# Gated cross-attention block: the turned query tile goes through memory instead of from SBUF to SBUF

## The chip, the cores and the metric

The kernel runs on one core of one Trainium2 chip. The metric is device time in microseconds (us) for one execution on that core. Three runs of the kernel before are given, and one further execution was taken by the hardware profiler. Engines are named as in the profile: PE (TensorE matmul), PEld (its weight loads), DVE (VectorE), ACT (ScalarE), POOL (GpSimd), SP (SyncE, which here only issues DMAs). All data is float32.

## The reference

There are 32 batches of 256 tokens with 256 features, and for each batch 77 context vectors. The first half of the block is a cross attention without softmax, with 8 heads of 128 features:

```python
f_q, f_k = proj(layernorm(x)), proj(ctx)           # heads x batch x tokens x 128; f_v is f_k
cosine   = f_q @ f_k.T / (|f_q| |f_k|)
variance = q_ratio * k_ratio                       # 2 min(var, 1) / (var + 1) of each feature vector
mixed    = cw * cosine + vw * cosine * decorr_scale + ww * variance
out      = (mixed @ f_v) @ w_out.T + b_out         # x += tanh(g_xattn) * out
```

The weights cw, vw, ww and decorr_scale are one number for each head, computed from all tokens. The second half is a self attention with 16 heads of 16 features, with the softmax over keys, two L2-normalised projections and a GELU, again gated and added to x.

To form f_q times f_k, PE needs both with the 128 features of a head on the partitions. Query features are made with tokens on the partitions, and so a tile of 128 tokens by 8 heads by 128 features has to be turned before it can be used.

## The kernel before

**Head.** The first part of the kernel (to about 170 us) reads all of x once for global statistics, prepares the weights and computes the first batches' features. Then comes a steady part, one cycle for each batch.

**Cycle.** A hand-written list names the stages of a cycle in their order; each entry says for which batch ahead of the current one a stage is run. The engines PE, ACT, DVE and POOL keep this order, since their instructions are recorded through a wrapper (line 30, which is why the profile puts nearly all work on L30). SP is not wrapped: a scheduler orders its DMAs by when their inputs are expected. The stages around the change, with n the cycle's batch:

```python
(2, turn_queries, 0),        # after mix_values(n, 1); then attend and ff_stats of n+1
(3, key_features),
(2, transpose_keys, 0),      # the reader of fv
(2, turn_queries, 1),        # near the end of the cycle
(3, measure_keys),
(3, align_keys),
(1, query_ratios),           # next cycle: n+2 is now n+1
(1, query_scores, 0),        # the reader of fqT: "mm<-fqT,fvT"
```

**Queries.** `query_features` makes fq, 128 tokens by 1024, for each of a batch's two token tiles (t = 0 and 1). `scale_queries` normalises it. `turn_queries` turns it into fqT, which has the 128 features of a head on the partitions. For the first two batches PE transposes; for the other 30, DVE transposes blocks of 32 by 32 into fb, and DMAs put the blocks in place: block row i of fb (partitions 32 i to 32 i + 31) and block column j go to partitions 32 j to 32 j + 31 of fqT. There is a single fqT buffer, and two buffers of fb. `query_scores` multiplies fqT by fvT; it needs both token tiles.

**Keys.** `key_features` computes key features in blocks of 128 context rows into one of four places of fvx, while a batch has 77 rows. So `align_keys` (lines 262 and 263) copies each batch's rows out of one or two blocks to partitions 0 to 76 of fv, by one DMA a piece, and their norms from nrx to nr:

```python
n = min(P - row, M - at)
nc.sync.dma_start(out=k["fv"][at : at + n], in_=fvx[i % 4][row : row + n])      # L262
nc.sync.dma_start(out=k["nr"][at : at + n], in_=nrx[row : row + n, i % 4, :])   # L263
```

The pieces have from 1 to 77 rows of 4 KB. There are two buffers of fv; a buffer's last reader is `transpose_keys` of the batch before the last ("mm<-dk,fv" in the trace).

**SP's queue.** All DMAs of the steady part are issued from SP, one after the other: the copies into fqT (L428), fv (L262), nr (L263), the output store of a batch (L626) and the load of x for a batch four ahead (L188). Eight semaphores are given out to the DMAs in turn, so SP issues a DMA only when the one eight places before it in that turn has landed.

Of the kernel before, what the change touches and what calls it, by code (L numbers as in the profile page):

```python
# [8 lines left out]
F32 = mybir.dt.float32  # L9
# [5 lines left out]
P = 128  # L15
H = 8
# [17 lines left out]
def gated_block_kernel(  # L34
# [24 lines left out]
    nc = tc.nc  # L59
# [8 lines left out]
    const = ctx.enter_context(tc.tile_pool(name="const", bufs=1))  # L68
    pa = ctx.enter_context(tc.tile_pool(name="pa", bufs=2))
    sw = ctx.enter_context(tc.tile_pool(name="sw", bufs=1))  # L70
    ps = ctx.enter_context(tc.tile_pool(name="ps", bufs=3, space=PSUM))
    ps_s = ctx.enter_context(tc.tile_pool(name="ps_s", bufs=2, space=PSUM))
    ps_z = ctx.enter_context(tc.tile_pool(name="ps_z", bufs=1, space=PSUM))
# [63 lines left out]
    def mm_tile():  # L137
        return ps.tile([P, 512], F32, tag="mm", name="mm")
# [263 lines left out]

    def turn_queries(b, t):

        k = kept[b]
        if t == 0:
            k["fqT"] = pa.tile([P, S // 32, H, 32], F32, tag="fqT", name="fqT", bufs=1)
        if b < 2:
            for hh in range(2):
                pt = mm_tile()  # L410
                for i in range(4):
                    h = hh * 4 + i
                    pe.transpose(
                        pt[:, i * P : (i + 1) * P], k["fq", t][:, h * P : (h + 1) * P], ident
                    )
                (act.copy if hh == 0 else dve.tensor_copy)(
                    k["fqT"][:, 4 * t : 4 * t + 4, hh * 4 : hh * 4 + 4, :],
                    pt.rearrange("p (h i a) -> p i h a", h=4, a=32),
                )
            return  # L420
        fb = pa.tile([P, 4, H, 32], F32, tag="fb", name="fb", bufs=2)
        dve.transpose(
            fb.rearrange("p j h a -> p h j a"),
            k["fq", t].rearrange("p (h j a) -> p h j a", j=4, a=32),
        )
        for i in range(4):
            for j in range(4):
                nc.sync.dma_start(  # L428
                    out=k["fqT"][32 * j : 32 * j + 32, 4 * t + i],
                    in_=fb[32 * i : 32 * i + 32, j],  # L430
                )

    def attend(b, t):

# [497 lines left out]
    for g in range(-2, NG):  # L932
# [9 lines left out]
        for i in range(4):  # L942
            k = 4 * g + i
# [179 lines left out]

    dve.tensor_scalar(dg[:, 1, :], ident[0:H, 0:H], lg[:, 2:3], 4.0, ALU.mult, ALU.mult)
    run(0, turn_queries, 0)
    pt = mm_tile()
    pe.matmul(
# [12 lines left out]
    for pair in (2, 0, 1):  # L1140
        run(0, key_outputs, pair)
    run(1, key_features)
    run(0, turn_queries, 1)
    run(0, query_ratios)
    for pair in range(3):
# [53 lines left out]
        (0, exponents, 2, 0),  # L1199
        (0, mix_values, 1),  # L1200
        (2, turn_queries, 0),
        (1, attend, 0),
        (1, ff_stats, 0),
# [69 lines left out]
```

## Time and profile before

| | |
|---|---|
| runs | 1469.19 us median of 3, from 1465.18 to 1469.28 |
| profiled execution | 1467.87 us, of which 1466.1 us is the span from first to last instruction |
| mean granted PE clock | 0.975 |
| issues of fqT<-fb on SP | 960 of 32 KB, median 589 ns on SP's queue |
| DVE transposes into fb | 60, median 1235 ns |
| matmuls on fqT or fvT (mm<-fqT,fvT) | 1024, median 379 ns |
| the SP queue's DMA share | 16.8% of 16 engines, 73.15 MB |

The page gives busy time by engine over the whole span, the chain of work that ended last, and the costliest groups of instructions. A busy share over the span is an average over the head and the steady part. More is told by windows that are cut at the same instruction of successive cycles, by the timelines of PE and SP in one such window, and by the list of who waited for whom. A wait for several semaphores is put down to the one that came last by the profile, so a DMA named there may stand for another DMA. The page prints no time to landing for these DMAs; where the text gives one, it is the last of the DMA's semaphore increments in the trace.

### The profile page before, as it was taken

To read this page: it belongs to the slowest core of one execution; us is meant where nothing else is said; L and a number is where in the kernel's file an instruction comes from. 1 tells how busy PE (TensorE), PEld (TensorE's weight loads), DVE (VectorE), ACT (ScalarE), POOL (GpSimd) and SP (SyncE) were. 2 spreads that over 40 slices of the span, in tenths; PEclk is the share of its full clock that TensorE was granted. 3 is DMA by queue.
4 is the path that set the end of the run, shared out by engine and by line. 5 is a ranking of instruction groups with operands and counts; after the bars stand their busy time and mean duration, and the time that the engine had idled before them with its cause. 6 is when DMAs were issued, how large, how long until landed. Compare 5 with 4: busy or idle time off the path is not lost.

```text
span 1466.1 us, 26809 instructions
## 1 busy us (share of the span) xinstructions
PE 1392.0 (95%) x8833; PEld 814.9 (56%) x8833; DVE 1057.0 (72%) x3053; ACT 905.5 (62%) x2978; POOL 533.4 (36%) x660
## 2 busy tenths in 40 slices
PE   6898899999999999999999899999999998999985
PEld 6764555555555555655555455555555554555541
DVE  5734678787777777777877686877878775878743
ACT  5712456667667666666666566766666664666675
POOL 5922333343333333343433233333433323333210
PEclk9989999999999999999999999999999998999996
DMA  8500011111111111111111111111111111111100
GB/s 267 176 15 27 3 45 46 42 51 43 49 47 49 46 54 47 59 49 40 51 43 45 42 49 49 56 46 51 45 44 49 47 41 40 47 42 35 32 19 15
DMA packets 72282, 74.87 MB, mean 51 GB/s; under 512 B 21370, under 2 KB 57135, under 8 KB 72142
## 3 DMA queue, kind: packets, MB, share of 16 engines
q1 hardware_dynamic: 71310, 73.15, 16.8%
q8 instruction: 70, 1.15, 0.3%
q14 instruction: 70, 0.57, 0.1%
q10 hardware_dynamic: 832, 0.00, 0.0%
HBM read 22.98 MB, written 8.39 MB: 21 GB/s over the span
## 4 chain that ended last, share of the span: by engine, by line
PE 69%; ACT 14%; DMA 4%; DVE 4%; issue 2%; SPq 1%; POOL 1%; ACTq 0%; POOLq 0%; DVEq 0%
PE mm L30 53%; PE sc L30 9%; ACT e L30 7%; PE zp L30 6%; ACT L30 4%; DMA fv<-fvx 4%; DVE nm L30 2%; SPq L428 1%; ACT u L30 1%; ACT fvx L30 1%; ACT dry L30 0%; ACT ge L30 0%; POOL rs L30 0%; DMA fqT<-fb 0%; DMA nr<-nrx 0%
## 5 line engine op out<-in xcount | busy, mean ns | idle before, releaser
L30 ACT ACTIVATE e<-sc,nm 128x256 f32<-128x256 f32 x1024 | 471.8, 484 | 200.5 <-DVE nm L30 200.4
L30 DVE TENSOR_REDUCE nm<-sc 128x4 f32<-128x1024 f32 x256 | 301.4, 1219 | 50.4 <-PE sc L30 50.4
L30 PE MATMUL mm<-winT,xTc 128*128 128x512 f32 x512 | 237.3, 605 | 2.6 <-DVE xTc L30 2.6
L30 ACT ACTIVATION_READ_ACCUMULATOR e<-sc,nm 128x1 f32 x1024 | 221.2, 216 | 0.0
L30 POOL TENSOR_TENSOR rq<-qt,nhalf 128x8 f32<-128x8 f32 x64 | 105.2, 1643 | 273.2 <-DVE qt L30 273.2
L30 PEld LDWEIGHTS mm<-winT,xTc 128*128 128x128 f32 x512 | 95.0, 191 | 120.7 <-issue 94.0
L30 PE MATMUL sc<-q,kTf 32*128 32x512 f32 x1024 | 153.9, 646 | 6.1 <-ACT e L30 6.1
L30 PE MATMUL mm<-vw,s 128*128 128x256 f32 x640 | 146.9, 384 | 0.0
L30 PE MATMUL zp<-e,vz 128*32 128x256 f32 x2048 | 140.0, 392 | 5.2 <-DVE vz L30 4.3
L30 POOL TENSOR_SCALAR i<-nn 128x2 f32<-128x2 f32 x64 | 14.0, 219 | 344.4 <-ACT ge L30 344.4
L30 PEld LDWEIGHTS mm<-vw,s 128*128 128x128 f32 x640 | 119.0, 190 | 28.5 <-issue 13.7
L30 POOL TENSOR_TENSOR fq<-fq,rq 128x1024 f32<-128x1024 f32 x64 | 121.3, 1896 | 5.0
L30 PE MATMUL mm<-w_of,zT 128*128 128x512 f32 x256 | 118.1, 605 | 0.8 <-DVE zT L30 0.8
L30 PEld LDWEIGHTS zp<-e,vz 128*32 128x32 f32 x2048 | 59.1, 111 | 95.7 <-issue 37.6
L30 PE MATMUL mm<-fqT,fvT 128*64 128x256 f32 (+2 forms) x1024 | 98.4, 396 | 13.2 <-DMA nr<-nrx 11.6
L30 DVE BATCH_NORM_STATS2 qst<-fq 128x6 f32<-128x128 f32 x512 | 104.7, 277 | 0.0
L30 PE MATMUL mm<-woutT,fvT 128*64 128x256 f32 (+2 forms) x1024 | 99.2, 384 | 0.6 <-DVE fvT L30 0.5
L30 POOL TENSOR_SCALAR rs<-mv 128x1 f32<-128x1 f32 x64 | 32.8, 512 | 169.5 <-DVE mv L30 135.4
L30 DVE RECIPROCAL sums<-sums 128x8 f32<-128x8 f32 x128 | 24.6, 192 | 92.6 <-ACT e L30 92.6
L30 ACT COPY vw<-mm 128x512 f32<-128x512 f32 x32 | 18.8, 586 | 115.6 <-PE mm L30 115.6
L30 PEld LDWEIGHTS mm<-fqT,fvT 128*64 128x64 f32 (+2 forms) x1024 | 48.7, 122 | 71.0 <-issue 51.9
L30 ACT ACT_TABLE_LOAD x64 | 82.1, 1283 | 7.4 <-DMA x<-in_x_dram 4.2
(204 smaller groups left out, 2316.8 us busy)
## 6 DMA issues: line engine op xcount, KB each, us to landing
fqT<-fb SPq DMA_DIRECT2D x960, 32.0 KB
x<-in_x_dram SPq DMA_DIRECT2D x64, 256.0 KB
out_dram<-x SPq DMA_DIRECT2D x32, 256.0 KB
fv<-fvx SPq DMA_DIRECT2D x13, 308.0 KB
ct<-in_ctx_dram SPq DMA_DIRECT2D x4, 512.0 KB
w_in_n<-in_L_xattn_w_in_dram SPq DMA_DIRECT2D x2, 512.0 KB
w_out_n<-in_L_xattn_w_out_dram SPq DMA_DIRECT2D x1, 1024.0 KB
ct<-in_ctx_dram SPq DMA_DIRECT2D x1, 384.0 KB
```

Of the source, the lines that this page charges most:

```text
L30: return lambda *args, **kw: self._tc.keep_in_program_order(method(*args, **kw))
L428: nc.sync.dma_start(out=k["fqT"][32 * j : 32 * j + 32, 4 * t + i], in_=fb[32 * i : 32 * i + 32, j],)
```

## The change

The blocks of fb no longer go straight to fqT. A pool of two buffers in memory (HBM) is added. Each tile is stored there in one DMA, fb with its 128 partitions by 4 KB as it lies, and is read back in four DMAs, one for each block column j: a read takes the 1 KB of column j of all 128 rows and lays row 32 i + p on partition p of the 32 partitions, at block i. The reads wait until the store has landed. The first two batches are as before. All else in the kernel's text is the same.

```diff
     sw = ctx.enter_context(tc.tile_pool(name="sw", bufs=1))
+    dram = ctx.enter_context(tc.tile_pool(name="dram", bufs=2, space=bass.MemoryType.DRAM))
...
             k["fq", t].rearrange("p (h j a) -> p h j a", j=4, a=32),
         )
-        for i in range(4):
-            for j in range(4):
-                nc.sync.dma_start(
-                    out=k["fqT"][32 * j : 32 * j + 32, 4 * t + i],
-                    in_=fb[32 * i : 32 * i + 32, j],
-                )
+        fd = dram.tile([P, 4, H * 32], F32, tag="fd", name="fd")
+        nc.sync.dma_start(out=fd, in_=fb.rearrange("p j h a -> p j (h a)"))
+        for j in range(4):
+            nc.sync.dma_start(
+                out=k["fqT"][32 * j : 32 * j + 32, 4 * t : 4 * t + 4].rearrange(
+                    "p i h a -> p i (h a)"
+                ),
+                in_=fd[:, j].rearrange("(i p) n -> p i n", p=32),
+            )
```

## The prediction

> **What bounds the kernel now.** I read the busy table first, then windows cut at the turns (from the end of one transpose into fb, t = 1, to the next), then the timelines of PE and SP where a cycle is long, and the chain there.
>
> ```profile
> PE 1392.0 (95%) x8833; PEld 814.9 (56%) x8833; DVE 1057.0 (72%) x3053; ACT 905.5 (62%) x2978; POOL 533.4 (36%) x660
> ```
>
> ```profile
> 724.33:764.29 39.96, 39.57 (x262) 22.91 (x261) 32.14 (x95) 26.46 (x89) 15.61 (x18) 1.00 0.17 50
> ...
> 805.10:851.64 46.54, 41.58 (x262) 23.78 (x261) 32.24 (x96) 26.57 (x89) 15.37 (x17) 0.93 0.15 45
> ...
> 1213.84:1263.72 49.88, 42.49 (x262) 24.12 (x261) 32.32 (x96) 26.57 (x89) 15.36 (x17) 0.90 0.12 37
> ```
>
> The columns are the window, its length, then busy time of PE, PEld, DVE, ACT and POOL, the granted clock, and DMA. An ordinary cycle is 39.96 us with PE busy 39.57 of it: nothing there can be won by a DMA. Two cycles of the same work take 46.54 and 49.88 us. In the longer one PE (first fence) stood idle 7.00 us before the first matmul on fqT, and SP (second) spent 20.01 us on the 16 copies of one tile, where 10 is usual:
>
> ```profile
> 1227.33 1.14 PE L30 MATMUL sc<-q,kTf 32*128 32x512 f32 x8
> 1235.47 5.52 PE L30 MATMUL mm<-fqT,fvT 128*64 128x256 f32 x32 [7.00 <-DMA nr<-nrx]
> ```
>
> ```profile
> 1199.60 11.22 SPq L428 DMA_DIRECT2D fqT<-fb  x16
> 1210.93 1.51 SPq L262 DMA_DIRECT2D fv<-fvx  x2
> 1213.87 20.01 SPq L428 DMA_DIRECT2D fqT<-fb  x16
> ```
>
> ```profile
> 1211.80 16.49 DMA fv<-fvx
> 1228.29 0.02 issue
> 1228.31 0.51 SPq L428
> ```
>
> The chain tells why: the second fv piece (71 rows) was 16.49 us under way, and the eighth copy went out only when it had landed at 1228.29. By the trace's semaphore increments the last copy landed at 1235.12, just ahead of PE's start, so PE waited for fqT; the nr that the row names landed after it (1235.85).
>
> The same two sources give every late turn (b of the queries that are turned):
>
> | b | slow fv piece, landed at | PE ready for fqT | PE waits | cycle longer by |
> |---|---|---|---|---|
> | 7 | 53 rows, 411.3 | 417.8 | 0.73 | 0.8 |
> | 12 | 74 rows | 619.1 | 0.04 | 0.1 |
> | 17 | 73 rows, 817.0 | 819.7 | 4.56 | 6.6 |
> | 19 | 47 rows, 899.1 | 906.1 | 0.88 | 0.9 |
> | 27 | 71 rows, 1228.3 | 1228.5 | 7.00 | 9.9 |
>
> Together 18.3 us. (Every fifth cycle, 40.81 us, has four matmuls more; that is work.) In the other turns the last copy lands 0.4 to 3.2 us before PE wants it.
>
> [...] 77 rows land in 3.4 us, 73 in 15.1, 47 in 10.7. [...] seven fqT copies issued behind the 71 rows, from 1213.87 on, land together between 1228.50 and 1229.60. [...] the granted clock is 0.93 and 0.90 in the two long cycles, and PE's busy time there is 2.0 and 2.9 us more for the same matmuls.
>
> **The change part by part.** The order of instructions on PE, ACT, DVE and POOL is the same in both programs; only SP's changes.
>
> *Removed:* 16 copies a tile, 60 tiles. Each holds SP 0.63 us (10.04 / 16), the last lands 1.84 us after its issue: 11.3 us from turn to landing, and SP is held for 10.
>
> *Added:* one store of 512 KB and four reads of 128 KB. Neither is in the trace; the nearest rows are an output store and the load that waits for it:
>
> ```profile
> 494.07 0.54 SPq L626 DMA_DIRECT2D out_dram<-x  x1
> 496.26 0.34 SPq L188 DMA_DIRECT2D x<-in_x_dram  x1
> ```
>
> The 256 KB store landed within 2.19 us. Loads of 256 KB in the head land 0.62 us apart, so twice the bytes make about 2.9 us (an estimate; bounds 2.2, and 6.5, which a 512 KB load of ct took in the crowded head). A 256 KB load alone lands 2.6 us after issue, a copy in 1.84, a load in the crowd in 3.5: I take 2.6 per read, bounds 1.8 and 3.5. Issues 0.6 us apart. Round trip: 2.9 + 0.1 + 3 x 0.6 + 2.6 = 7.4 us, with SP held for 5.4.
>
> *Moved, t = 0:* fqT of t = 0 has over 25 us of room, so its landing is worth nothing. But SP then goes on to fv, 4.6 us sooner, and now fv's own conditions decide. In the b = 27 cycle these are ACT's copies into fvx (start 1204.72, 1.03 long) for the first piece and PE's last reading of the old fv (1204.77, 1.92 long) for the second: 1206.7, where it was issued at 1211.80. Where there is one piece, only the second condition holds.
>
> *Moved, t = 1:* in cycles with two pieces the program puts both nr copies between store and reads. They wait for nrx, ready 4.2 us after the turn (POOL, 405.64 + 1.66 against 403.13), and take SP 1.6: reads begin at 5.9, land at 5.9 + 1.8 + 2.6 = 10.3. PE wants fqT about 14.5 us after the turn, so this is covered; were the cover gone, the cost would be the excess. The output store and x load behind it come no later than before (old release 10.1, new 8.3).
>
> *The late turns.* The store has 8 of its 128 rows on the engine that fv occupies[...]: 8/71 of 16.49 is 1.9 us, less the fixed part, 1.6. Then reads: 0.1 + 1.8 + 2.6 = 4.5. So fqT lands 6.1 us after fv, where the nine copies left took 6.8.
> - b = 27: fv lands 16.49 after 1206.7, 1223.2; fqT 1229.3; PE ready 1228.5: 0.8 us wait left, about 1.1 us with the slower clock.
> - b = 17: the same offset gives issue 797.9 instead of 801.94, fv 813.0, fqT 819.1 against 819.7: none.
> - b = 7: fv 407.5, fqT 413.6 against 417.8: none.
> - b = 19: one piece, issue about 883.9 instead of 888.45, fv 894.6, fqT 900.7 against 906.1: none.
> - b = 12: none.
>
> Gain 18.3 - 1.1 = 17.2 us. What is late next is PE itself. The DMA engines' load rises from 16.8% by 31 MB on 73: no bound. Against the profiled execution, 1467.87 us (span 1466.1 and 1.8 around it), this is 1450.7; the median shown, 1469.19, is 1.3 higher, so I predict 1451.
>
> **Rivals.**
> - *SP is not free sooner.* If store and reads of t = 0 hold SP for the old 10 us (store at its upper bound 6.5, and reads that issue slowly), fv stays where it was and only the tail shrinks from 6.8 to 6.1: b = 7, 12 and 19 are cured (1.8 us), b = 17 and 27 get 0.7 x 1.4 each: 3.8 us, 1464. For it: no such store is in the trace. Against: the 2.19 us row. Chance 0.10.
> - *No gain.* The tail after fv is longer than 6.8 us by as much as fv is earlier (each read at 3.5, store slow behind fv, 4 us more): 1468. Chance 0.05.
> - *Slower: the round trip outlasts the room in every cycle.* From 14.5 us after a t = 1 turn on, each microsecond costs all 30 turns one, and more by the clock. At 16 us: 1.5 x 30 = 45 us, 1513. It needs a store of 6.5 us and reads that do not overlap (4 x 2.6 = 10.4). For it: 32 destination partitions of 1 KB pieces from memory are unseen. Against: copies with the same destination overlap freely now. Chance 0.05.
> - That the change does not do what it says is not open: SP's order shows the store and four reads in each turn.
>
> **How the numbers follow.** Main case 0.80, from 1446 (all 18.3 gained, and the lowest of the runs shown) to 1457 (reads at 3.5 and store 1 us later: b = 27 keeps 3 us, b = 17 about 2). The range 1446 to 1463 takes in most of the first rival. A difference of 0.3%, 4.4 us, is about what a measurement of this kernel can tell from no change. Faster 0.88 (main, and most of the first rival), same 0.07, slower 0.05.
>
> **What would show it.** Right: windows at b = 17 and 27 near 40 and 41 us with the clock at 1.00; fv issued 7 us after the t = 0 turn; fd landing about 3 us after issue, reads about 2.6; PE's waits for DMA in the steady part under 2 us instead of 13. Wrong: PE idle before fqT in ordinary cycles; SP held over 8 us by the t = 0 turn; fqT landing over 8 us after a one-engine fv.

## The result, and the profile after

The changed kernel takes 1453.15 us (median of 4 runs, 1451.74 to 1454.22), against 1467.18 us for the kernel before (4 runs, the three above and one more, 1464.3 to 1469.28). The ratio is 0.9892, with a 95% interval from 0.9873 to 0.9911: faster by 1.1%. The profiled execution took 1451.74 us, with a span of 1450.0 us, 16.1 us less than the span before.

Three places of the profile after answer to those shown above. First the windows, cut at the turns of the same batches (b = 15, 17 and 27; window, length, busy time of PE, PEld, DVE, ACT and POOL, granted clock, DMA share, GB/s):

```profile
724.27:764.33 40.06, 39.38 (x262) 22.88 (x261) 32.15 (x95) 26.50 (x89) 15.73 (x18) 1.00 0.22 70
805.13:845.11 39.98, 39.59 (x262) 22.91 (x261) 32.16 (x97) 26.49 (x89) 15.36 (x17) 1.00 0.25 79
1206.32:1247.36 41.04, 39.66 (x262) 23.11 (x261) 32.35 (x97) 26.50 (x89) 15.36 (x17) 1.00 0.21 73
```

The ordinary cycle is what it was. The long one at b = 17 has become an ordinary one (46.54 to 39.98 us), the one at b = 27 has 1.1 us left of its 9.9, and the clock is no longer lowered in either. Next, SP in the cycle of b = 27, from the t = 0 turn on:

```profile
1192.04 0.32 SPq L429 DMA_DIRECT2D fd<-fb  x1
1194.69 1.74 SPq L431 DMA_DIRECT2D fqT<-fd  x4
1197.80 2.05 SPq L263 DMA_DIRECT2D fv<-fvx  x2
1206.35 0.34 SPq L429 DMA_DIRECT2D fd<-fb  x1
1210.51 1.40 SPq L264 DMA_DIRECT2D nr<-nrx  x2
1216.63 2.71 SPq L431 DMA_DIRECT2D fqT<-fd  x4
```

The turn of t = 0 now holds SP from 1192.04 to 1196.43, 4.4 us, where it was 11.2. After that SP waits for the conditions of fv (its source written, its old contents read), and fv no longer waits for SP: the second fv piece went out 7.2 us after the turn instead of 12.3. And PE at the same place:

```profile
1219.82 1.14 PE L30 MATMUL sc<-q,kTf 32*128 32x512 f32 x8
1221.94 2.93 PE L30 MATMUL mm<-fqT,fvT 128*64 128x256 f32 x32 [0.99 <-DMA fqT<-fd]
```

The wait is 0.99 us instead of 7.00, and the matmuls after it take 2.93 us instead of 5.52. The chain there still goes through the slow fv piece, under another name: the store of the tile stands behind it. By the semaphore increments the fv piece landed at 1215.22 and the store at 1216.55. The trace's packets show the same: the last 4 KB of fv started at 1214.62, and behind it eight 4 KB packets of the store, one after another, from 1214.78 to 1215.87.

```profile
1206.35 10.20 DMA fd<-fb
...
1218.91 2.79 DMA fqT<-fd
1221.70 0.24 issue
1221.94 2.93 PE mm L30 x32
```

In all of the steady part PE waits 1.0 us for fqT, where it waited 13.2. These are the lines of its list of waits, first before, then after (the nr of the first line stands for fqT, as the prediction worked out for b = 27):

```profile
PE mm L30 <- DMA nr<-nrx: 11.6, 2, 7.0
PE mm L30 <- DMA fqT<-fb: 1.6, 2, 0.9
```

```profile
PE mm L30 <- DMA fqT<-fd: 1.0, 1, 1.0
```

A good measure of the steady part alone is the time from the first to the last DVE transpose into fb, which the view of that tile gives, again before and after:

```profile
L30 DVE STREAM_TRANSPOSE fb<-fq x60: 1234/1235/1245, 187.1 to 1382.3; 128x1024 f32<-128x1024 f32 x60
```

```profile
L30 DVE STREAM_TRANSPOSE fb<-fq x60: 1234/1235/1236, 187.7 to 1365.8; 128x1024 f32<-128x1024 f32 x60
```

That is 1195.2 and 1178.1 us, or 17.1 us less.

### The profile page after: what moved, and what is told of

Same layout as the page of the kernel before. It is cut to its first block, busy times and chain, and to the rows that moved or that the text cites. A ratio compares the mean times of both kernels' runs of the same rounds, so it can differ in the third digit from the quotient of the medians.

```text
span 1450.0 us, 25957 instructions
## 1 busy us (share of the span) xinstructions
PE 1387.5 (96%) x8833; PEld 812.5 (56%) x8833; DVE 1056.7 (73%) x3053; ACT 906.3 (63%) x2978; POOL 534.5 (37%) x660
## 3 DMA queue, kind: packets, MB, share of 16 engines
q1 hardware_dynamic: 68430, 104.56, 22.2%
## 4 chain that ended last, share of the span: by engine, by line
PE 72%; ACT 14%; DVE 5%; issue 2%; DMA 1%; POOL 1%; SPq 0%; ACTq 0%; POOLq 0%
PE mm L30 56%; PE sc L30 10%; ACT e L30 7%; PE zp L30 7%; ACT L30 4%; DVE nm L30 3%; ACT u L30 1%; ACT fvx L30 1%; DMA fd<-fb 1%; POOL rs L30 0%; ACT dry L30 0%; DVE fb L30 0%; DVE qst L30 0%; DMA fqT<-fd 0%; ACT ge L30 0%
## 5 line engine op out<-in xcount | busy, mean ns | idle before, releaser
L30 PEld LDWEIGHTS mm<-vw,s 128*128 128x128 f32 x640 | 119.0, 190 | 28.5 <-issue 13.7
L30 PE MATMUL mm<-fqT,fvT 128*64 128x256 f32 (+2 forms) x1024 | 93.9, 383 | 1.0 <-DMA fqT<-fd 1.0
L30 POOL TENSOR_SCALAR xn<-x,mv_x,rstd_x 128x256 f32<-128x256 f32 x64 | 78.9, 1239 | 10.3 <-issue 10.3
```

The source lines that it names most:

```text
L30: return lambda *args, **kw: self._tc.keep_in_program_order(method(*args, **kw))
```

## The experiments

My theory was that the late turns came from fv pieces that lie on one DMA engine or a few, and that the change helped mainly because the short hold of SP by the t = 0 tile let these pieces go earlier. The trace of the kernel before has such pieces: the 4 KB packets of the 47 rows went one after another, 0.155 us apart (median), and so did the last of the 71 rows, with a DMA share of 0.06, one engine of 16, at 26 GB/s from 1219.9 to 1224.9. Of the seven fqT copies issued behind those 71 rows, each had 15 of its 16 semaphore increments by 1219.98, and the sixteenth only between 1228.50 and 1229.60. Why these row counts and not others go this way is not shown. The rivals were that the shorter turn of t = 1 pays by itself, and that fewer DMAs or the memory route pay tile by tile. Each ratio below is to the kernel before, run beside it on the same chip; the median of the kernel before lay between 1467.18 and 1469.10 us, so compare ratios rather than medians. The stretch is the one between first and last transpose. "fv cut" means that each fv piece goes in two DMAs, a multiple of 16 rows and the rest.

| kernel | median us | ratio (95%) | stretch | PE waits for fqT, steady |
|---|---|---|---|---|
| before | 1467.18 | 1 | 1195.2 | 13.2 |
| changed | 1453.15 | 0.9892 (0.9873, 0.9911) | 1178.1 | 1.0 |
| t = 0 alone through memory | 1454.49 | 0.9905 (0.9886, 0.9923) | 1178.4 | 1.7 |
| t = 1 alone through memory | 1462.74 | 0.9969 (0.9954, 0.9984) | 1189.6 | 8.5 |
| before, fv cut | 1446.85 | 0.9855 (0.9834, 0.9876) | 1177.4 | 0 |
| changed, fv cut | 1446.14 | 0.9850 (0.9831, 0.9869) | 1176.7 | 0 |
| changed, fv cut in the head alone | 1447.73 | 0.9858 (0.9833, 0.9883) | 1177.7 | 0.7 |
| changed, fv cut after the head alone | 1452.31 | 0.9887 (0.9866, 0.9908) | 1176.6 | 0 |
| changed, two stores a tile | 1477.48 | 1.0059 (1.0043, 1.0076) | 1203.6 | 22.2 |
| changed, fv cut, two stores a tile | 1461.14 | 0.9943 (0.9929, 0.9958) | 1189.9 | 12.4 |
| changed, fv cut, three stores at t = 1 | 1595.24 | 1.0862 (1.0844, 1.0880) | 1318.7 | 102.0 |

(The last column is PE's idle time right before its first matmul on fqT, summed over the 30 cycles. PE's list of waits puts part of it down to nr, to the load of x or to "issue". In each of these cycles fqT landed later than PE was ready, or within 0.2 us of it.)

### One half of the change at a time

The first kernel has `t == 0` as the condition, the second `t == 1`. The lines under the condition are those of the change, indented.

```diff
+        if t == 0:
             fd = dram.tile([P, 4, H * 32], F32, tag="fd", name="fd")
             nc.sync.dma_start(out=fd, in_=fb.rearrange("p j h a -> p j (h a)"))
...
+        else:
+            for i in range(4):
+                for j in range(4):
+                    nc.sync.dma_start(
+                        out=k["fqT"][32 * j : 32 * j + 32, 4 * t + i],
+                        in_=fb[32 * i : 32 * i + 32, j],
+                    )
```

**The t = 0 tile alone.**

> The change for the t = 0 tile alone; t = 1 keeps its 16 copies. My theory (late turns come from fv pieces on one DMA engine; the change helps because the short hold of SP at t = 0 lets fv go some 5 us sooner): nearly the whole gain stays. fv of b = 27 lands about 1215.2 as in the changed kernel, the nine copies left take 6.8, so PE waits about 1.1 us there and nowhere else: 18.3 - 1.6 = 16.7 us faster than before, within 1 us of the changed kernel. Rival A (the shorter t = 1 turn itself is what pays): little gain, under 5 us. Rival B (the count of DMAs or the memory route as such pays, tile by tile): half the gain, 8 us.

Measured: the stretch is 16.8 us shorter than before, and the total is 0.13% above the changed kernel's, with overlapping intervals. Nearly all of the gain comes from the tile of t = 0, whose landing PE never waited for. SP in the cycle of b = 27, then PE:

```profile
1191.82 0.32 SPq L430 DMA_DIRECT2D fd<-fb  x1
1194.43 1.74 SPq L432 DMA_DIRECT2D fqT<-fd  x4
1197.57 2.08 SPq L263 DMA_DIRECT2D fv<-fvx  x2
1206.13 14.97 SPq L441 DMA_DIRECT2D fqT<-fb  x16
```

```profile
1222.47 2.93 PE L30 MATMUL mm<-fqT,fvT 128*64 128x256 f32 x32 [1.73 <-DMA nr<-nrx]
```

The 16 copies of t = 1 are still held up behind fv (14.97 us), but fv started early enough for that to cost 1.73 us instead of 7.00 (1.1 was expected).

**The t = 1 tile alone.**

> The change for the t = 1 tile alone; t = 0 keeps its 16 copies. My theory: fv goes out as late as in the kernel before, only the tail behind it shrinks: b = 7, 12 and 19 cured (1.8 us), b = 17 waits 3.0 instead of 4.6 (2.3 us with the clock), b = 27 6.4 instead of 7.0 (0.8): about 4.9 us faster than before. Rival A (shorter t = 1 turn pays): nearly the whole gain, 14 to 17 us. Rival B: half, 8 us.

Measured: 5.6 us less in the stretch, 0.31% in the total. fv is nearly as late as before (its second piece goes out 11.7 us after the t = 0 turn, 12.3 before), since 16 copies of t = 0 stand in front of it, and PE pays:

```profile
1200.93 10.72 SPq L441 DMA_DIRECT2D fqT<-fb  x16
1211.75 1.52 SPq L263 DMA_DIRECT2D fv<-fvx  x2
1215.20 0.33 SPq L430 DMA_DIRECT2D fd<-fb  x1
1219.36 1.40 SPq L264 DMA_DIRECT2D nr<-nrx  x2
1230.11 1.75 SPq L432 DMA_DIRECT2D fqT<-fd  x4
```

```profile
1234.86 4.45 PE L30 MATMUL mm<-fqT,fvT 128*64 128x256 f32 x32 [5.04 <-DMA fqT<-fd]
```

That 5.6 us is close to the 4.9 expected is in part luck. At b = 17 PE still waits 3.41 us (3.0 expected), and yet its cycle gains only 0.2 us (2.3 expected), since PE is busy there for 42.51 us where it was 41.58 before, with the clock at 0.93 in both. At b = 27 the wait falls to 5.04 us (6.4 expected) and the cycle gains 3.3 us (0.8 expected).

The two halves together rule out both rivals. The shorter turn of t = 1 is worth 5.6 us alone and almost nothing once fv goes early (17.1 against 16.8), and tile by tile the gain is as unequal as it could be.

### The slow piece itself

```diff
-            nc.sync.dma_start(out=k["fv"][at : at + n], in_=fvx[i % 4][row : row + n])
+            cut = n // 16 * 16
+            for lo, hi in ((0, cut), (cut, n)):
+                if lo < hi:
+                    nc.sync.dma_start(
+                        out=k["fv"][at + lo : at + hi], in_=fvx[i % 4][row + lo : row + hi]
+                    )
```

**On the kernel before**, with its 16 copies a tile.

> The kernel before, with each fv piece cut into a multiple of 16 rows and the rest, so that none lies on one engine or few; the 16 copies stay. My theory: the slow pieces land in under 5 us and all late turns go: 18.3 us faster than before, PE's waits for DMA in the steady part under 1 us, a little better than the changed kernel. Rival A or B (what was lost lies in the 16 copies themselves): no gain, 0 us, or slower by the issues added.

Measured: 17.8 us less in the stretch, and the total falls to 0.9855. By the trace's semaphore increments the 71 rows of b = 27, now 64 and 7, land in 3.1 and 2.9 us, where they took 16.5. SP in that cycle holds fqT for no longer than in any other:

```profile
1190.40 10.68 SPq L433 DMA_DIRECT2D fqT<-fb  x16
1201.18 2.77 SPq L265 DMA_DIRECT2D fv<-fvx  x4
1204.66 10.05 SPq L433 DMA_DIRECT2D fqT<-fb  x16
```

PE does not wait for a DMA anywhere in the steady part. So the 16 copies were not the trouble by themselves: with the fv pieces cut, the old route is as fast as the new one (0.9855 and, in the next run, 0.9850).

**On the changed kernel.**

> The changed kernel with the fv pieces cut in the same way. My theory: what is left at b = 27 (0.99 us of waiting) goes, about 1.4 us faster than the changed kernel, the same time as the kernel before with the cut: the two remedies do not add up. Rivals A and B: they add up, the time is below the changed kernel by 10 us or more if the cut alone brings as much.

Measured: the remaining wait is gone and the stretch is 1.4 us shorter, as expected; the total is that of the kernel before with the cut. The remedies do not add up, because they take away the same waits. But the total fell more than the stretch: 0.9850 against 0.9892 is some 6 us, and I had expected 1.4. Hence two more runs, with the cut for the first two batches alone (`if b < 2`) and for the others alone.

> The changed kernel with the fv pieces of the first two batches alone cut. The cut of all pieces brought more than the 1.5 us that the steady part shows. My theory: the rest is in the head, where POOL's wait for the first nr falls from 4.6 to 1.5 us (the 51 rows of fv on three engines stand in front of it) and PE waits behind it: about 3 us faster than the changed kernel, 0.987 of the kernel before. Rival (the head only varies with PE's clock from run to run): no difference, 0.989.

> The changed kernel with the fv pieces cut from the third batch on. My theory: b = 27 alone is cured, 1.4 us faster than the changed kernel, 0.988 of the kernel before, and the first POOL wait for nr stays at 4.6 us. Rival: all of the 6 us that the full cut brought is here, 0.985.

Measured: 0.9858 with the cut in the head alone, 0.9887 with it in the steady part alone. The head's share is about 5 us, the steady part's about 1. The place is POOL's wait for the first nr, which stands behind the 51 rows of fv (in the changed kernel they landed in 7.2 us, from 120.3 to 124.1 mostly two or three 4 KB packets at a time, where the 52 rows of a later batch took 3.7); first the changed kernel, then the one cut in the head:

```profile
POOL nr L30 <- DMA nr<-nrx: 4.6, 1, 4.6
```

```profile
POOL nr L30 <- DMA nr<-nrx: 1.5, 1, 1.5
```

PE shows what this costs, again the changed kernel and then the one cut in the head:

```profile
127.29 2.08 PE L30 MATMUL mm<-dk,fv 77*128 77x96 f32 x16 [1.75 <-issue]
129.16 3.56 PE L30 MATMUL mm<-winT,xTc 128*128 128x512 f32 x4
```

```profile
125.42 2.06 PE L30 MATMUL mm<-dk,fv 77*128 77x96 f32 x16
127.32 1.91 PE L30 MATMUL mm<-winT,xTc 128*128 128x512 f32 x4
```

The idle 1.75 us is gone, and the four matmuls that follow take 1.91 us instead of 3.56. Together with 0.4 us in the stretch this makes 3.8 us, of 4.3 between the two profiled executions and about 5 between the ratios. The rest, about one microsecond, is not explained: in the head the granted clock differs from one execution to the next (0.83 to 0.94 from 80 to 110 us in four of these profiles), ahead of any instruction that differs.

### How much round trip is covered

The prediction's worst case said that a round trip is free up to some 14.5 us after the t = 1 turn, and then costs every cycle. To try this, the tile was copied once or twice more, from memory to memory, before it is read. The first diff is that of the two kernels with two stores, where it holds for both tiles; the second is that of the kernel with three, where it holds for t = 1 alone:

```diff
+        fe = dram.tile([P, 4, H * 32], F32, tag="fe", name="fe")
+        nc.sync.dma_start(out=fe, in_=fb.rearrange("p j h a -> p j (h a)"))
         fd = dram.tile([P, 4, H * 32], F32, tag="fd", name="fd")
-        nc.sync.dma_start(out=fd, in_=fb.rearrange("p j h a -> p j (h a)"))
+        nc.sync.dma_start(out=fd, in_=fe)
```

```diff
         nc.sync.dma_start(out=fd, in_=fb.rearrange("p j h a -> p j (h a)"))
+        for hop in range(2 * t):
+            fe = dram.tile([P, 4, H * 32], F32, tag=f"fe{hop}", name="fe")
+            nc.sync.dma_start(out=fe, in_=fd)
+            fd = fe
```

> The changed kernel with the tile stored twice: from fb to memory, then from memory to memory, then read. That puts some 3 us more into each of the 60 round trips, and holds SP that much longer. My theory: PE wants fqT 14.5 us after the turn, a round trip of 7 to 10.4 us plus 3 is still covered, so ordinary turns cost nothing; only those behind a one-engine fv pay: b = 27 waits about 5 us and b = 17 about 3 us, together some 10 us slower than the changed kernel, near the kernel before. Rival (the length of the round trip itself sets the cycle): 30 turns of t = 1 by 3 us, 90 us slower.

> The same second store on the kernel with the fv pieces cut. My theory: no late turn is left that could pay, so the time is that of the changed kernel with the cut, within 1 us. Rival (the round trip sets the cycle): 90 us slower.

> The kernel with the fv pieces cut, and two more stores (memory to memory) in the t = 1 turns alone. My theory, with a room of 14.5 us: in the 13 cycles with one key block no nr copies stand before the next store, fqT lands 2.6 + 2 x 3.3 + 4.5 = 13.7 us after the turn, no wait; in the 17 with two, the second store waits for nr (5.9), fqT lands at 5.9 + 6.6 + 5.1 = 17.6 and PE waits some 3 us each, with a slower clock behind it: 17 x 3 x 1.3 = 66 us slower than with the cut alone (bounds 40 and 110). Rival (all is covered, PE is never late): no loss. Rival (each microsecond of the round trip is paid): 30 x 6.6, about 200 us.

Measured: with two stores the changed kernel loses some 24 us (1.0059 against 0.9892) and the one with the cut some 14, where I expected 10 and nothing; with three stores at t = 1 the loss is 149 us where 66 was expected. All three miss to the same side, mainly for one reason: I had priced the copy from memory to memory at 3 to 3.3 us, and by the semaphore increments it mostly takes 3.9 to 4.6. In cycles with two pieces of keys this copy also stands behind the two nr copies, so it begins only about 6 us after the turn. SP with three stores in the cycle of b = 8, which has two pieces (L437 comes after the nr copies), then PE at its end, then the windows of this cycle and of the next, which has one piece:

```profile
469.71 0.35 SPq L434 DMA_DIRECT2D fd<-fb  x1
473.88 1.54 SPq L269 DMA_DIRECT2D nr<-nrx  x2
475.52 0.52 SPq L437 DMA_DIRECT2D fe<-fd  x1
476.13 0.52 SPq L640 DMA_DIRECT2D out_dram<-x  x1
479.99 0.51 SPq L437 DMA_DIRECT2D fe<-fe  x1
480.61 0.51 SPq L189 DMA_DIRECT2D x<-in_x_dram  x1
484.33 1.75 SPq L440 DMA_DIRECT2D fqT<-fe  x4
```

```profile
489.18 5.25 PE L30 MATMUL mm<-fqT,fvT 128*64 128x256 f32 x32 [4.85 <-DMA fqT<-fe]
```

```profile
469.69:516.90 47.21, 41.96 (x262) 23.85 (x261) 32.32 (x95) 26.61 (x89) 15.64 (x18) 0.93 0.27 83
516.90:558.78 41.88, 39.56 (x262) 23.04 (x261) 29.60 (x78) 26.49 (x89) 13.97 (x17) 1.00 0.32 99
```

PE was ready at 489.18 - 4.85 = 484.33, which is 14.6 us after the turn; the next cycle, with one piece, gives 14.5. So the room was right, and the three misses are misses of prices. With three stores there is a second one: fqT mostly landed 15.4 to 16.0 us after the turn in cycles with one piece, where 13.7 was expected, so these pay too, and a long wait cost 1.5 us for each microsecond instead of the 1.3 that I took.

The runs also bear on the rivals I set against them. The loss is not 90 us for 3 us more, and it appears only past the room. With the cut and two stores, 13 of the 17 cycles with two pieces wait, those whose fqT lands 14.8 to 16.2 us after the turn; the four where it lands after 14.0 to 14.2 don't, nor do those with one piece, where it lands after 11.5 to 13.1. (b = 30, with one piece that arrives late, waits 0.1.)

## Why the prediction was right

**The bound and the late turns.** Right. Ordinary cycles did not change, and of the five late turns the four that were to be cured are cured. One reading was off without harm: at b = 7 the landing at 411.3 is that of the 75 rows issued behind the 53, which landed at 410.5.

**The prices.** The 512 KB store landed in 2.6 us (2.9 was estimated), and it held SP's sequencer for 0.32. The first read of a tile lands in 2.6 us, as taken, the later three in 2.9 to 3.1; the reads issue 0.47 us apart (0.6 taken), and the first goes out 0.1 us after the store has landed, as taken. The round trip of t = 1 is mostly 7.0 us in cycles with one piece of keys (7.4), and 10.4 with two, where nr stands between (10.3): the errors have both signs and come to less than half a microsecond. SP is held 4.4 us at t = 0 (5.4); the full microsecond did not matter, since fv was by then waiting for its own conditions.

**fv sooner.** The second piece of b = 27 went out 7.2 us after the turn, as worked out from PE's last reading of the old fv. This step carries the result, and the run with t = 0 alone shows it by itself.

**The tail behind fv.** At b = 27 the last read landed 6.5 us after fv (6.1): the store came 1.3 after fv (1.6; that 8 of its 128 rows would stand behind fv had not been shown, and eight packets did), the reads then took 5.2 (4.5), since one of their issues took 1.41 us. That the sum still held is in part luck: fv itself was 0.5 us less under way than before (16.01 against 16.49). At b = 17 the tail was 5.7. So the wait of b = 27 was 0.99 us (0.8) and its cycle 1.1 us too long (1.1).

**The sum.** 17.2 us were predicted for the steady part, 17.1 measured. The profiled execution gained 16.1, since its head and end are together 1.0 us longer; whether the change has a part in that is not shown. The medians are 14.0 apart, for two reasons that lie outside the steady part: the profiled execution of the changed kernel is the fastest of its four, 1.4 us below their median, and the kernel before, run once more, came in at 1464.3 us, which lowered its median by 2. The total also holds a slip: 1450.7 for the profiled execution and 1.3 more for the median make 1452, not the 1451 that was named. The median came out at 1453.15.

**The rivals.** SP was free sooner, against the first. The tail was shorter and not longer, against the second. The third, that the round trip outlasts the room, was not met by this change but was made to happen with added stores, and its threshold stood. Its price was too low for long waits: I reckoned one microsecond for each late one, and a little for the clock. In the run with three stores, 102.0 us of waiting lengthened the stretch by 142 us (1318.7 - 1176.7), 1.4 for one.

**What the prediction did not see.** It put the late turns down to a few slow fv pieces and yet weighed only the change at hand. The cause it named could be removed at its root, by cutting the pieces, for more than the change brought (0.9855 against 0.9892).

## What to carry to other kernels

When a transfer lands late, look at what stands before it in its queue and on its DMA engines before making it shorter: here 17 us of the steady part hung on a handful of copies (71, 73, 47 and 53 rows) that took 10.7 to 16.5 us to land, and cutting each at a multiple of 16 rows (the 71 rows then landed in 3.1 and 2.9 us) did more than rerouting all the traffic behind them (0.9855 against 0.9892). A change to a step that nobody waits for can carry nearly the whole gain (here 16.8 of 17.1 us), if that step holds the queue through which the late one is issued. And a longer path was free only up to its room, here 14.5 us, which can be read beforehand as the time from the event that starts it to the moment its reader is ready.

## What the hardware showed that was not expected

- A store of 512 KB from SBUF lands in 2.6 us and a 128 KB read from memory in 2.6 to 3.1, but a copy of 512 KB from memory to memory mostly takes 3.9 to 4.6 us, half as long again as the store or more.
- SP's time to issue a DMA is not the same for all: 0.32 to 0.35 us for a store of 128 rows of 4 KB, 0.43 for a read of 128 pieces of 1 KB (0.31 for the first of four), 0.59 for a copy of 32 rows of 1 KB. Of these three the smallest was the dearest to issue.
- A microsecond of idle PE cost more than itself in long waits, and hardly more in short ones. In the run with three stores, 11 cycles with waits of 1.3 to 2.0 us were 1.05 us longer for each microsecond of waiting, and 18 cycles with waits of 3.2 to 5.1 us were 1.5 us longer for each (against the same cycles of the changed kernel with the cut). Over the whole run the mean granted clock was 0.945 instead of 0.982. With the cut and two stores, 12.4 us of waits, none above 2.1, lengthened the stretch by 13.2. In the windows above, a wait of 4.85 us went with a clock of 0.93, and one of 1.96 us left it at 1.00.
- The price of a long wait does not follow its length alone. With t = 1 alone through memory, the cycle with 3.41 us of waiting was 6.4 us too long, and the one with 5.04 us was 6.6 (granted clock 0.93 and 0.96).
